# A two-layer graph-attention kernel: layer 2's softmax of large tiles in two halves, and the next tile's softmax six rows later

## The chip, the cores and the metric

The kernel runs on one core of one Trainium2 chip. The metric is the device time of one execution, in microseconds (us). Engines are named as the profile does: PE (matrix products), DVE (VectorE), ACT (ScalarE), POOL (GpSimd) and SP (the queue that issues plain transfers). PEld is PE's loading of weights.

## The reference

A graph with 10,000 nodes of 768 features and 170,000 directed edges (80,000 pairs in both directions and a loop on each node) goes through two attention layers. In each, a node's new row is a weighted sum of the rows of its neighbours:

```python
xl = (x @ W).reshape(n, heads, out_ch)
alpha_src = jnp.einsum('nhc,hc->nh', xl, a_src)
alpha_dst = jnp.einsum('nhc,hc->nh', xl, a_dst)
e = jax.nn.leaky_relu(alpha_src[src] + alpha_dst[dst], 0.2)
m = jax.ops.segment_max(e, dst, num_segments=n)
e = jnp.exp(e - m[dst])
s = jax.ops.segment_sum(e, dst, num_segments=n)
alpha = e / (s[dst] + 1e-16)
out = jax.ops.segment_sum(xl[src] * alpha[:, :, None], dst, num_segments=n)
```

Layer 1 has 4 heads of 256 features, layer 2 has one head of 768. After each layer comes a layer norm; layer 1 then has relu and adds `h0 @ Wr1 + br1`, layer 2 adds `h1 @ Wr2 + br2`. The input is added at the end, and a last layer norm follows. Everything is float32.

## The kernel before

The kernel first computes layer 1's table of rows and sorts the nodes by their number of incoming edges. The sorted nodes are cut into 79 tiles of 128 nodes; each node has one partition. A tile has as many *slots* as its busiest node has edges: 41, 27, 26, 25, 24, 24, 23 and so on down to 8. One slot is one row for each of the 128 nodes: a gather of 128 rows of 770 numbers (394 KB) from the table in HBM. The program keeps two paths; for this input the ordered one runs (`ordered_layer1`, then `ordered_layer2`).

`TURNS` sets the order in which tiles are worked: first every second tile from the smallest to the largest, then the others from large to small. I call the place in this order the *position*, t in the code of layer 2. Its slots go 8, 10, 11, 12, ... 22, 22, 23, 24 (position 37), 26 (38), 41 (39), 27 (40), 25 (41), 24, 23, 22, ... 9. In all there are 1377 slots.

The change is in layer 2 alone. There, a `Ring` in SBUF holds 41 rows (`RING2`). `ring.fetch(upto)` issues the gathers in order of slots: a tile's first row (the nodes' own rows) as a plain transfer on SP, all others as indirect transfers on POOL (L424). A slot of the ring can be filled again only when everything that reads its old row is done.

Position t of the loop does the following; the order of instructions on every engine is that of the Python text (`manual_schedule`), and each engine works its own list in order.

- `residual(t + 1)`: PE multiplies the next tile's `h1` by `Wr2` into a PSUM tile `rs[t + 1]` of two banks (L949, L952), and adds x by an identity product.
- `weights_of(t + 1)` is a generator that the loop starts in the middle of tile t. Its first part, `logits`, has DVE compute e for all slots of the tile (L477 reads the scores out of the ring's rows, then L188, L481, L484) and ACT its Exp (L485). Its second part has DVE normalise e (`normalised`, L496 to L499, after `doubled`, L502). Then for each row ACT makes a diagonal matrix of e (L937; 5 buffers of 4 diagonals), and PE multiplies it with columns 512 to 767 of the row (L938), summing in the free quarter of `rs[t + 1]`. A bias product (L933) goes before.
- Columns 0 to 511 are summed by DVE: one instruction for each row, `acc = row * e + acc` (L519, `weigh`), starting from the bias at the first row. After each, `ring.fetch` lets POOL issue one more gather.
- `norms(t - 1)`, the layer norms of the tile before, is stepped through at rows 0, 3, 6 and 9: statistics by DVE (L577, L579), `sd` by two ACT instructions (L581, L582), the scaling (L591, L593), the second norm, and the output row (L968), which POOL writes by an indirect transfer (L970).

The row at which the next tile's softmax starts is `turn`; its normalising stands three rows (`LEAD`) later:

```python
if t + 1 < NT and SLOTS[t + 1] + LEAD <= ring.size:
    ahead = weights_of(t + 1)
    turn = min(max(n // 3, n + SLOTS[t + 1] + 2 * LEAD - ring.size), n - LEAD)
```

The last gather of tile t + 1 is allowed by row `n + SLOTS[t + 1] - 41 - 1` of tile t, so the term in the middle puts the softmax six rows behind that. For the 41-row tile the condition fails: its weights are computed after the last row of the tile before.

Of the kernel before, what the change touches and what calls it, by code (L numbers as in the profile page):

```python
# [28 lines left out]
F32 = mybir.dt.float32  # L29
I32 = mybir.dt.int32  # L30
BF16 = mybir.dt.bfloat16
AF = mybir.ActivationFunctionType
OP = mybir.AluOpType
AX = mybir.AxisListType

P = 128
# [16 lines left out]
ON_PE1 = 4  # L53

# [25 lines left out]
def gnn_kernel(ctx, tc, x, x_cols, src, dst, src_col, dst_col, W1, a_src1, a_dst1, b1, g1, be1, Wr1, br1,  # L80
# [797 lines left out]
    def ordered_layer2():  # L878
        nonlocal ps_big
        with tc.tile_pool(name="b2", bufs=1) as pool, tc.tile_pool(name="small2", bufs=2) as small, \  # L880
# [39 lines left out]
            def whole(t):  # L920
                return SLOTS[t] <= ring.size

            def weights_of(t):


                n = SLOTS[t]
                ad = small.tile([P, H2], F32, name="ad")
                nc.vector.tensor_add(ad, ring.slot(FIRST[t])[:, C2:C2 + H2], lift)
                e, _ = logits(small, ring, FIRST[t], FIRST[t] + n, ad, H2, C2)
                yield e  # L930
                normalised(small, e, H2, t)
                to = rs[t][:, C2:2 * C2 - ON_PE2]
                nc.tensor.matmul(to, ones, b2_b[0:1, ON_PE2:], start=False, stop=False, skip_group_check=True)  # L933
                for k in range(n):
                    if k % G == 0:
                        diagonals = pool.tile([P, G, P], F32, name="diagonals", bufs=DIAGONALS)
                    nc.scalar.activation(diagonals[:, k % G, :], ident, AF.Copy, scale=e[:, k, :])  # L937
                    nc.tensor.matmul(to, diagonals[:, k % G, :], ring.slot(FIRST[t] + k)[:, ON_PE2:C2],  # L938
                                     start=False, stop=(k == n - 1), skip_group_check=True)
                yield  # L940

# [36 lines left out]
            ready = []  # L978
            assert all(whole(t) for t in range(NT))
            for t in range(NT):  # L980
# [4 lines left out]
                e = (ready or list(weights_of(t)))[0]  # L985
# [6 lines left out]
                if t + 1 < NT and SLOTS[t + 1] + LEAD <= ring.size:  # L992

                    ahead = weights_of(t + 1)
                    turn = min(max(n // 3, n + SLOTS[t + 1] + 2 * LEAD - ring.size), n - LEAD)
                for k in range(n):
                    if k in (turn, turn + LEAD):
                        ready += itertools.islice(ahead, 1)
                    if k in (LEAD, 2 * LEAD, 3 * LEAD):
                        next(last, None)  # L1000
                    weigh(acc, ring.slot(FIRST[t] + k), e[:, k], ON_PE2, None if k else b2_b)
# [3 lines left out]
                ready += ahead  # L1005
# [280 lines left out]
```

## Time and profile before

| | us |
|---|---|
| median of 3 runs | 5645.9 (5635.85 to 5646.04) |
| the profiled execution | 5629.25 |
| its span, first to last instruction | 5627.4 |
| busy in the span: PE, DVE, POOL, ACT | 4889.5, 4288.7, 3236.3, 2810.9 |
| L424, gathers of both layers, 2675 | 2655.8 (993 ns each) |
| L519, row times weight plus sum, 2530 | 1578.4 (624 ns each, two shapes) |
| L938, PE's part of the rows, 2754 passes | 742.1 (428 ns each) |

The profile is one execution's record. Its slices cut the span into 40 equal parts of 141 us; each digit is a share in tenths. Layer 2 fills the last fifteen and a half. A line of the timeline has the start, the length, the engine, the line of the kernel and the operation, then output<-inputs, the number of instructions merged into the line, and in brackets how long the engine had been idle and what ended that. A line of the waits has engine, its line, what it waited for, then the sum, the number of waits and the longest. PE's ends are modelled, so a wait "for PE" is read by the waiting engine's start, not by PE's record. "issue" and "remote" name idle time for which the record shows no instruction that ended it.

### The profile page before, as it was taken

The page shows a single profiled execution, that of the slowest core. Times are in us where ns is not written, and L with a number is a line of the kernel's source. Part 1 is how long each engine was busy: PE and PEld are TensorE (multiplying, and loading weights), DVE is VectorE, ACT ScalarE, POOL GpSimd, SP SyncE. Part 2 cuts the span into 40 slices and gives each one's busy share as a digit, 9 for nine tenths or more (in the row PEclk, how much of TensorE's full clock was granted, in tenths as well). Part 3 has the DMA queues.
Part 4 walks back from the last instruction along what each step waited for, and adds up shares of the span by engine and source line. Part 5 has one row for each costly group of instructions (what it writes and reads, how often), then busy time and mean ns, then how long its engine had stood idle before and what let it go on. Part 6 is the DMA issues. An engine that isn't in the chain of part 4 may idle for free. (4 is left out here: it accounts for less than half of the span.)

```text
span 5627.4 us, 59568 instructions
## 1 busy us (share of the span) xinstructions
PE 4889.5 (87%) x15191; PEld 2895.8 (51%) x15191; DVE 4288.7 (76%) x7729; ACT 2810.9 (50%) x8184; POOL 3236.3 (58%) x3159
## 2 busy tenths in 40 slices
PE   8999996999999875789999999998887747788898
PEld 3444443555555543455555555565555534555565
DVE  5783344999998887888999995887676656767787
ACT  3443343777788776778877763332222222222232
POOL 2447364556666555566665543666565656666663
PEclk9999998999999987899999999998888878889999
DMA  4333626999999987899999986998888878888885
GB/s 155 122 99 87 92 89 243 327 338 350 361 363 364 347 318 263 317 346 357 366 356 354 337 292 246 330 337 313 294 301 286 282 242 291 307 300 305 304 328 201
DMA packets 474306, 1591.37 MB, mean 283 GB/s; under 512 B 118327, under 2 KB 122487, under 8 KB 473958
## 3 DMA queue, kind: packets, MB, share of 16 engines
q0 software_dynamic: 322384, 1286.62, 64.5%
q1 hardware_dynamic: 149520, 297.43, 15.7%
q10 hardware_dynamic: 2054, 3.42, 0.2%
q8 instruction: 128, 2.10, 0.1%
q14 instruction: 220, 1.80, 0.1%
HBM read 1431.80 MB, written 177.29 MB: 286 GB/s over the span
## 5 line engine op out<-in xcount | busy, mean ns | idle before, releaser
L424 POOL DMA_INDIRECT ring<-table,slots x2675 | 2655.8, 993 | 1791.0 <-issue 518.8
L519 DVE SCALAR_TENSOR_TENSOR acc<-ring,e,acc 128x512 f32<-128x512 f32 (+1 forms) x2530 | 1578.4, 624 | 148.0 <-PE acc L733 48.6
L508 ACT ACTIVATE ring<-ring,e 128x256 f32<-128x256 f32 x3284 | 1338.6, 508 | 1.4 <-issue 1.4
L515 DVE TENSOR_TENSOR acc<-acc,ring 128x1024 f32<-128x1024 f32 x801 | 985.6, 1230 | 71.4 <-DVE acc L519 1.4
L952 PE MATMUL big<-wr,w 128*128 128x512 f32 (+1 forms) x2464 | 878.9, 502 | 139.8 <-issue 137.9
L938 PE MATMUL big<-ring,diagonals 128*128 128x256 f32 x2754 | 742.1, 428 | 206.0 <-issue 159.2
L171 PE MATMUL big<-w,xT 128*128 128x512 f32 x1896 | 825.9, 597 | 27.0 <-DMA w<-in_W_dram 10.4
L171 PE MATMUL big<-wr,xT 128*128 128x512 f32 x1896 | 833.5, 596 | 0.2 <-issue 0.2
L826 PE MATMUL half<-w,hT 128*128 128x512 f32 (+1 forms) x2528 | 830.4, 486 | 0.0
L938 PEld LDWEIGHTS big<-ring,diagonals 128*128 128x128 f32 x2754 | 586.4, 216 | 364.9 <-issue 232.7
L952 PEld LDWEIGHTS big<-wr,w 128*128 128x128 f32 x2464 | 482.3, 197 | 499.9 <-issue 468.9
L937 ACT ACTIVATE diagonals<-ident,e 128x128 f32<-128x128 f32 x1377 | 424.3, 388 | 617.2 <-remote 227.0
L826 PEld LDWEIGHTS half<-w,hT 128*128 128x128 f32 x2528 | 477.8, 189 | 372.3 <-issue 333.2
L733 PE MATMUL acc<-ring,diagonals 128*128 128x256 f32 x1912 | 481.8, 410 | 209.4 <-ACT diagonals L727 203.8
L171 PEld LDWEIGHTS big<-w,xT 128*128 128x128 f32 x1896 | 362.0, 192 | 486.6 <-issue 466.3
L171 PEld LDWEIGHTS big<-wr,xT 128*128 128x128 f32 x1896 | 356.7, 192 | 420.6 <-issue 420.5
L733 PEld LDWEIGHTS acc<-ring,diagonals 128*128 128x128 f32 x1912 | 388.8, 206 | 295.4 <-ACT diagonals L727 225.0
L581 ACT ACTIVATE sd<-mv,eps 128x1 f32<-128x1 f32 x237 | 69.4, 293 | 709.9 <-DVE mv L579 398.4
L727 ACT ACTIVATE diagonals<-ident,e 128x128 f32<-128x128 f32 x956 | 293.0, 387 | 204.2 <-DVE e L499 171.9
L665 DVE TENSOR_TENSOR scr<-big,ad_b 128x1024 f32<-128x1024 f32 x79 | 96.7, 1224 | 379.9 <-ACT row L662 348.1
L670 POOL TENSOR_TENSOR row<-row,none 128x1024 f32<-128x1024 f32 x79 | 187.1, 2368 | 266.6 <-ACT row L662 264.6
L485 ACT ACTIVATE e<-e 128x68 f32<-128x68 f32 (+29 forms) x160 | 38.2, 239 | 567.0 <-DVE e L484 302.0
(173 smaller groups left out, 3635.0 us busy)
## 6 DMA issues: line engine op xcount, KB each, us to landing
ring<-table,slots POOLq DMA_INDIRECT x2675
table<-row SPq DMA_DIRECT2D x79, 516.0 KB
h_d<-hT SPq DMA_DIRECT2D x79, 512.0 KB
w<-h_d SPq DMA_DIRECT2D x77, 512.0 KB
table<-row SPq DMA_DIRECT2D x79, 385.0 KB
ring<-table SPq DMA_DIRECT2D x79, 385.0 KB
xT<-in_x_cols_dram SPq DMA_DIRECT2D x79, 384.0 KB
x_d<-xt SPq DMA_DIRECT2D x79, 384.0 KB
```

Source lines behind the costliest of these rows:

```text
L171: nc.tensor.matmul(p[:, c:e], aT[:, j, :], w[:, j, c:e], start=(j == 0), stop=(j == k - 1))
L424: nc.gpsimd.indirect_dma_start(out=to, out_offset=None, in_=table, in_offset=bass.IndirectOffsetOnAxis(ap=index, axis=0), **more)
L508: nc.scalar.activation(row[:, s], row[:, s], AF.Copy, scale=e[:, h:h + 1])
L515: nc.vector.tensor_add(acc[:, :c], acc[:, :c], row[:, :c])
L519: nc.vector.scalar_tensor_tensor(acc[:, s], row[:, s], e[:, h:h + 1], (acc if first is None else first)[:, s], op0=OP.mult, op1=OP.add)
L670: nc.gpsimd.tensor_add(row[:, :C1], row[:, :C1], b1_b)
L727: nc.scalar.activation(diagonals[:, k * H1 + i, :], ident, AF.Copy, scale=e[:, k, i:i + 1])
L733: nc.tensor.matmul(acc[:, c:d], diagonals[:, k * H1 + i, :], ring.slot(q + k)[:, c:d], start=(k == 0 and c % BANK == 0), stop=(k == m - 1 ...
L826: nc.tensor.matmul(q, hT[:, j, :], w2[:, j, c:c + q.shape[1]], start=(j == 0), stop=(j == K1 - 1))
L937: nc.scalar.activation(diagonals[:, k % G, :], ident, AF.Copy, scale=e[:, k, :])
L938: nc.tensor.matmul(to, diagonals[:, k % G, :], ring.slot(FIRST[t] + k)[:, ON_PE2:C2], start=False, stop=(k == n - 1), skip_group_check=True)
L952: nc.tensor.matmul(r[:, c:d], hT[:, j, :], wr2[:, j, c:d], start=False, stop=(j == K1 - 1 and d < C2), skip_group_check=True)
```

## The change

Tiles of 26 and more rows (`PARTED2`: positions 38, 39 and 40 with 26, 41 and 27 rows) get their softmax in two halves with a running maximum. The first half's weights are exponentials under the first half's maximum, not normalised. Before row `cuts[1]` of the tile itself, `logits` of the second half takes the maximum of both; `fade` = exp(old maximum - new one) scales what was summed so far: DVE scales `acc` (and adds the bias there), ACT scales PE's quarter of `rs[t]` in place in PSUM. The second half's weights and the fade carry the whole sum's reciprocal. The second half's logits stand three rows before the cut, the normalising one row before.

For all tiles `turn` gets `4 * LEAD` in place of `2 * LEAD`, needs only the next tile's first half in the ring (`cuts_of(t + 1)[1]`), and stands behind the tile's own cut. The condition on the ring's size is gone, so the 41-row tile's first half is computed in the loop of the 26-row tile.

```diff
@@ -51,6 +51,7 @@
 ON_PE2 = 512
 SHARE = 4
 ON_PE1 = 4
+PARTED2 = 26
 
 
 def chunk_counts(n_edges):
@@ -917,27 +918,58 @@
             ones = pool.tile([1, P], F32, name="ones")
             nc.vector.memset(ones, 1.0)
 
-            def whole(t):
-                return SLOTS[t] <= ring.size
+            def cuts_of(t):
+
+                n = SLOTS[t]
+                return [0, n // 2, n] if n >= PARTED2 else [0, n]
 
             def weights_of(t):
 
 
-                n = SLOTS[t]
+                n, at, cuts = SLOTS[t], FIRST[t], cuts_of(t)
                 ad = small.tile([P, H2], F32, name="ad")
-                nc.vector.tensor_add(ad, ring.slot(FIRST[t])[:, C2:C2 + H2], lift)
-                e, _ = logits(small, ring, FIRST[t], FIRST[t] + n, ad, H2, C2)
-                yield e
-                normalised(small, e, H2, t)
+                nc.vector.tensor_add(ad, ring.slot(at)[:, C2:C2 + H2], lift)
                 to = rs[t][:, C2:2 * C2 - ON_PE2]
-                nc.tensor.matmul(to, ones, b2_b[0:1, ON_PE2:], start=False, stop=False, skip_group_check=True)
-                for k in range(n):
-                    if k % G == 0:
-                        diagonals = pool.tile([P, G, P], F32, name="diagonals", bufs=DIAGONALS)
-                    nc.scalar.activation(diagonals[:, k % G, :], ident, AF.Copy, scale=e[:, k, :])
-                    nc.tensor.matmul(to, diagonals[:, k % G, :], ring.slot(FIRST[t] + k)[:, ON_PE2:C2],
-                                     start=False, stop=(k == n - 1), skip_group_check=True)
+
+                def summed(e, lo, hi):
+                    for k in range(lo, hi):
+                        if (k - lo) % G == 0:
+                            diagonals = pool.tile([P, G, P], F32, name="diagonals", bufs=DIAGONALS)
+                        nc.scalar.activation(diagonals[:, (k - lo) % G, :], ident, AF.Copy, scale=e[:, k - lo, :])
+                        nc.tensor.matmul(to, diagonals[:, (k - lo) % G, :], ring.slot(at + k)[:, ON_PE2:C2],
+                                         start=False, stop=(k == n - 1), skip_group_check=True)
+
+                def add_b2():
+                    nc.tensor.matmul(to, ones, b2_b[0:1, ON_PE2:], start=False, stop=False, skip_group_check=True)
+
+                e, top = logits(small, ring, at, at + cuts[1], ad, H2, C2)
+                yield {0: (e, None)}
+                if len(cuts) == 2:
+                    normalised(small, e, H2, t)
+                    add_b2()
+                else:
+                    doubled(e, t)
+                    total = small.tile([P, H2], F32, name="total")
+                    nc.vector.reduce_sum(total, e.rearrange("p k h -> p h k"), axis=AX.X)
+                summed(e, 0, cuts[1])
                 yield
+                for lo, hi in zip(cuts[1:], cuts[2:]):
+                    e, new = logits(small, ring, at + lo, at + hi, ad, H2, C2, top)
+                    fade = small.tile([P, H2], F32, name="fade")
+                    nc.vector.tensor_sub(fade, top, new)
+                    nc.scalar.activation(fade, fade, AF.Exp)
+                    yield
+                    part = small.tile([P, H2], F32, name="part")
+                    nc.vector.reduce_sum(part, e.rearrange("p k h -> p h k"), axis=AX.X)
+                    nc.vector.scalar_tensor_tensor(total, total, fade, part, op0=OP.mult, op1=OP.add)
+                    nc.vector.tensor_scalar(total, total, 1e-16, None, op0=OP.add)
+                    nc.vector.reciprocal(total, total)
+                    nc.vector.tensor_mul(fade, fade, total)
+                    nc.vector.tensor_mul(e, e, total[:, None, :].to_broadcast([P, hi - lo, H2]))
+                    nc.scalar.activation(to, to, AF.Copy, scale=fade)
+                    add_b2()
+                    summed(e, lo, hi)
+                    yield lo, (e, fade)
 
             def residual(t):
 
@@ -975,34 +1007,51 @@
             q = product(brT, wr2, C2)
             rs = {0: residual(0)}
             last = iter(())
-            ready = []
-            assert all(whole(t) for t in range(NT))
+            ready, ahead = [], iter(())
+            assert max(SLOTS) <= ring.size
             for t in range(NT):
                 n = SLOTS[t]
                 if 0 < t < NT - 1:
                     rs[t + 1] = residual(t + 1)
                 h = parts[4 + t % 2][:, :C2]
-                e = (ready or list(weights_of(t)))[0]
+                if not ready:
+                    ahead = weights_of(t)
+                    ready += itertools.islice(ahead, 2)
+                es, later, cuts = dict(ready[0]), ahead, cuts_of(t)
                 acc = ps_acc.tile([P, BANK], F32, name="acc")
                 if not t:
                     rs[1] = residual(1)
                     ring.fetch(RING2)
                 next(last, None)
                 ready, ahead, turn = [], iter(()), n
-                if t + 1 < NT and SLOTS[t + 1] + LEAD <= ring.size:
+                if t + 1 < NT:
 
                     ahead = weights_of(t + 1)
-                    turn = min(max(n // 3, n + SLOTS[t + 1] + 2 * LEAD - ring.size), n - LEAD)
+                    turn = min(max(n // 3, cuts[-2] + 1, n + cuts_of(t + 1)[1] + 4 * LEAD - ring.size), n - LEAD)
                 for k in range(n):
+                    if k + LEAD in cuts[1:-1]:
+                        next(later)
+                    if k + 1 in cuts[1:-1]:
+                        lo, es_lo = next(later)
+                        es[lo] = es_lo
                     if k in (turn, turn + LEAD):
                         ready += itertools.islice(ahead, 1)
                     if k in (LEAD, 2 * LEAD, 3 * LEAD):
                         next(last, None)
-                    weigh(acc, ring.slot(FIRST[t] + k), e[:, k], ON_PE2, None if k else b2_b)
+                    lo = max(c for c in es if c <= k)
+                    weights, fade = es[lo]
+                    row = ring.slot(FIRST[t] + k)
+                    if k == 0 and len(cuts) > 2:
+                        nc.vector.tensor_scalar(acc[:, :ON_PE2], row[:, :ON_PE2], weights[:, 0], None, op0=OP.mult)
+                    else:
+                        if k == lo and fade is not None:
+                            nc.vector.scalar_tensor_tensor(acc[:, :ON_PE2], acc[:, :ON_PE2], fade, b2_b[:, :ON_PE2],
+                                                           op0=OP.mult, op1=OP.add)
+                        weigh(acc, row, weights[:, k - lo], ON_PE2, None if k else b2_b)
                     ring.fetch(FIRST[t] + k + 1 + ring.size)
                     if t + 2 < NT and k == n // 2:
                         ins[t + 2] = fetch_x(t + 2)
-                ready += ahead
+                ready += itertools.islice(ahead, 2 - len(ready))
                 for _ in last:
                     pass
                 if not t:
```

## The prediction

> **What bounds the kernel now.** I read the page's slices first: layer 2 fills the span from 3.45 ms on, and in its middle PE falls from 9 to 4 tenths. The change acts only there, so I then read the stretch tile by tile (edges: first row product L519 of positions 34 to 41). Columns: stretch, length; then busy us and count of PE, PEld, DVE, ACT, POOL; granted clock, DMA share, GB/s.
>
> ```profile
> 4316.20:4350.30 34.10, 26.97 (x87) 18.13 (x86) 23.52 (x47) 8.78 (x28) 21.90 (x23) 0.85 0.85 295
> 4350.30:4386.00 35.70, 27.96 (x97) 19.16 (x95) 23.37 (x46) 8.77 (x28) 23.61 (x25) 0.86 0.86 301
> 4386.00:4423.40 37.40, 26.80 (x78) 18.18 (x78) 24.24 (x47) 10.24 (x33) 22.07 (x24) 0.77 0.83 286
> 4423.40:4461.30 37.90, 20.76 (x62) 12.26 (x61) 25.16 (x48) 7.61 (x24) 26.43 (x28) 0.76 0.93 327
> 4461.30:4520.20 58.90, 43.87 (x135) 27.83 (x135) 26.91 (x51) 5.92 (x19) 26.24 (x28) 0.79 0.73 208
> 4520.20:4583.50 63.30, 25.06 (x97) 20.75 (x96) 37.75 (x64) 18.61 (x62) 35.75 (x38) 0.67 0.73 249
> 4583.50:4631.40 47.90, 31.40 (x98) 21.44 (x97) 27.32 (x52) 12.05 (x40) 24.96 (x27) 0.79 0.71 245
> 4631.40:4665.30 33.90, 24.59 (x74) 14.47 (x72) 25.66 (x49) 8.96 (x29) 23.09 (x24) 0.80 0.94 321
> ```
>
> The rows per tile are 22, 22, 23, 24, 26, 41, 27, 25. The three tiles of 26 and more rows (lines 5 to 7) move 208 to 249 GB/s where their neighbours move 286 to 327. Next the ordinary cycle, from the timeline of 4300 to 4345:
>
> ```profile
> 4307.17 5.95 ACT L937 ACTIVATE diagonals<-ident,e 128x128 f32<-128x128 f32 x20 [3.02 <-PE big L952]
> ...
> 4313.54 0.69 PE L933 MATMUL big<-b,ones 1*128 1x256 f32 x2
> ...
> 4327.68 0.69 ACT L937 ACTIVATE diagonals<-ident,e 128x128 f32<-128x128 f32 x2 [14.56 <-PE big L938]
> 4327.79 0.95 POOL L424 DMA_INDIRECT ring<-table,slots  x1 [3.74 <-PE big L938]
> ...
> 4328.82 1.02 DVE L593 SCALAR_TENSOR_TENSOR w<-w,sd,be 128x768 f32<-128x768 f32 x1 [9.32 <-ACT sd L582]
> ```
>
> ACT has 20 diagonal buffers; the last two of 22 diagonals wait for PE, and behind them stand the two sd instructions for which DVE waits 9.32 us. All three engines come free together at 4327, just after POOL's run of gathers stopped at 4324. So an ordinary tile is POOL issuing 1.25 us a row (0.95 busy and 0.30 between) and then a pause until PE's results arrive. DVE (23.5 busy of 34.1) and PE (27 of 34.1) have room. Seven ordinary tiles (positions 33 to 35 and 44 to 47: 151 rows, 234 us, counted the same way) give the pause: 234 - 151 x 1.25 = 45 us, 6.5 a tile. Then the waits from position 37 to 41, and DVE and PE around the 41-row tile:
>
> ```profile
> DVE e L477 <- DMA ring<-table,slots: 59.6, 6, 13.8
> POOL ring L424 <- DVE acc L519: 34.5, 17, 14.9
> POOL ring L424 <- PE big L938: 27.2, 7, 13.7
> DVE w L593 <- ACT sd L582: 26.5, 3, 10.1
> ```
> ```profile
> 4494.29 0.15 DVE L928 TENSOR_TENSOR ad<-ring,lift 128x1 f32<-128x1 f32 x1
> 4507.16 0.22 DVE L477 TENSOR_TENSOR e<-ring,ad 128x35 f32<-128x35 f32 x1 [12.72 <-DMA ring<-table,slots]
> 4516.77 0.17 DVE L477 TENSOR_TENSOR e<-ring,ad 128x6 f32<-128x6 f32 x1 [9.38 <-DMA ring<-table,slots]
> ```
> ```profile
> 4519.56 20.49 PE L938 MATMUL big<-ring,diagonals 128*128 128x256 f32 x82 [6.38 <-ACT diagonals L937]
> 4539.98 0.69 PE L933 MATMUL big<-b,ones 1*128 1x256 f32 x2
> 4578.91 9.90 PE L938 MATMUL big<-ring,diagonals 128*128 128x256 f32 x36 [38.24 <-issue]
> ```
>
> The 41-row tile fills the whole ring: its softmax can't start until the last row of the tile before it is used up, so DVE stands 22 us, POOL meanwhile has nothing to fetch (14.9 us), and then POOL waits 13.7 us more for PE. The 27-row tile's softmax comes after row 33 of 41, so PE idles 38 us.
>
> **The change, part by part.** All sums are against the profiled execution (5629.25 us, span 5627.4). It lies 16.7 us below the median of the runs shown (5645.9); I put the difference onto the median.
>
> *Two halves for 26, 41 and 27 rows.* The 41-row tile now needs 20 rows in the ring at row 17 of the 26-row tile, and 41 only at its own row 17, some 13 us (17 x 0.78) after the last slot came free. The 22 us of DVE and the 38 us of PE lose their cause. What is late next is POOL's own cadence. Positions 37 to 41 are 143 rows: 143 x 1.25 + 5 x 6.5 = 211 us, against 37.9 + 58.9 + 63.3 + 47.9 + 33.9 = 241.9 now. Gain 31 us. DMA allows it: 143 rows of 394 KB and five tiles of 1.29 MB in and out are 62.8 MB, in 211 us 298 GB/s, below the 327 of line 4.
>
> *What the halves add.* Per tile some 11 small DVE instructions (0.15 to 0.2 each, rows L477 to L499) and one 128x512 pass over acc (0.78): 3 us, hidden under POOL while DVE has 8 us of waiting in a tile; uncovered they would cost 9 us for three tiles. On ACT one more Exp of e, an Exp of fade and the scaling of PSUM: below 0.3, 0.3 and about 0.5 us (L508's 128x256 is 508 ns). The scaling is the dear one: it waits for PE's first half, and behind it on ACT stand the second half's diagonals and the next tile's Exp, for which DVE waits. PE's bias product waits for it too, and POOL then for PE's release of rows. No row shows this wait. From below it is 0: PE has a residual (10.7 us in the ordinary tile) between the halves. From above it is another pause, 6.5 a tile, 20 for three. As PE's results came only when POOL paused (14.56 us for ACT above), I take half: 10 us.
>
> *Next tile's softmax six rows later.* The term goes from 6 to 12 rows after the last fetch. With max(n // 3, ...) it moves 13 tiles by six rows (positions 31 to 36 and 40 to 46; 20 to 27 rows), some twenty others of 17 to 21 rows by one to five, and none of 16 or fewer; positions 37 and 39, whose next tile is parted, come 7 and 8 rows earlier, and 38 gets a place in the loop. POOL's and SP's instructions keep their order exactly; what moves past row products are DVE's logits and normalising, ACT's Exp and diagonals, PE's L933 and L938. Six rows are 6 x 0.78 = 4.7 us. It takes away DVE's waits at L477 in the ordinary tiles, but POOL runs through these, so they pay only where POOL stopped as well: positions 36, 42 and 43 lie 2.2, 0.6 and 1.4 us above 1.25 n + 6.5. Gain 4. Its price is PE's slack. Diagonals begin at 4307.17 and PE turns to them at 4313.54: 6.4 us of slack, 1.7 left after the move. Positions 36 and 44 had 2 to 3 us and come about 2 us late; PE makes that up in its wait. From below 0, from above 4.7 us x 13 = 61 if no slack holds; I take 2, by the row shown.
>
> A rule against this part: the Trainium skill, "DMA: Bandwidth & Descriptors", Anatomy of one DMA, fits a GpSimd-issued transfer at 2.0 us plus bytes over 436 GB/s. That would be 2.9 us for 394 KB (an estimate from that page), so six rows would be ample and the move worth nothing, the 4 us above being 0. The trace differs: the last gather before L477's 4516.77 was issued at 4506.56, 10.2 us earlier, behind a queue of others.
>
> Sum: -31 + 10 - 4 + 2 = **-23 us**: 5606 on the profiled execution, **5623 on the median**, 0.4%.
>
> **The rivals.**
> *A: the second pause is paid in full, and once more in the 41-row tile.* For: POOL ran 38 gathers in the 41-row tile while PE's work was long done; now rows 20 to 40 are released only after the scaling. Against: the residual between. Time: -31 + 20 + 6.5 - 4 + 2 = -6, 5640, no change to tell.
> *B: slower, by PE's slack.* One mechanism: the later diagonals reach PE after its residual, and L938, and the rows it releases to POOL, run late in each of the 13 tiles. It decides once diagonals come later than 6.4 us; from there each us costs 13. At the full 4.7 a tile: +61 - 23 = +38, 5684; at half, +8, 5654. For: positions 36 and 44 have only 2 to 3 us. Against: POOL's pause, not PE, ends those tiles, and PE's crawl before 4327 is waiting that can absorb it. The skill's "TensorE: Matmul & The Clock Gate", What's actually happening, would make it worse: an idle window of about 3.4 us halves the clock. The granted clock agrees (0.67 in the tile with 38 us of idle, 0.85 in the ordinary one).
> *C: the gain is larger.* If the waits at tile ends shrink too because PE's work is spread more evenly (clock 0.85 instead of 0.67 to 0.79), each of the ten tiles of 21 to 25 rows saves up to 2.5 us: -23 - 25 = -48, 5598.
> *D: the change doesn't act, since the first half waits as well.* At row 17 of 26 the last needed row was asked for 12 row products ago: 9.4 us against 10.2, so at most 1 us is left. Counted with A.
>
> **How the numbers follow.** About 0.2% (11 us) is what this kernel's measurement can tell from no change. Forecast 0.50, C 0.11, A with D 0.21, B 0.18. Faster: forecast and C, 0.61, plus a little of A, 0.62. Slower by more than 11 us is most of B and the worst of A: 0.17. Within: 0.21. The range runs from C with a few us of scatter (5594) to halfway into B (5666); about 0.1 lies above and 0.05 below. The forecast's own range is 5606 to 5635.
>
> **What would show it.** Right: DVE's wait for DMA at the logits line falls from 59.6 us at these positions to under 10; the 38 us gap of PE before the 27-row tile is gone; the 41-row tile keeps POOL above 0.85 of its cadence; positions 37 to 41 take 210 to 225 us. Wrong by A: ACT's scaling waits over 5 us for PE in each parted tile, and POOL waits for PE after some 20 gathers. Wrong by B: PE waits for ACT's diagonals after its residual in positions 31 to 46, and tiles of 20 to 25 rows, now 32 to 38 us, grow by 2 us or more.

## The result, and the profile after

| | kernel before | changed kernel |
|---|---|---|
| median, us | 5641.66 (5635.85 to 5646.04) | 5610.27 (5600.19 to 5623.55) |
| profiled execution, us | 5629.25 | 5608.18 |
| its span, us | 5627.4 | 5606.3 |

The ratio is 0.995, with a 95% interval of 0.9933 to 0.9968: the changed kernel is 31 us faster by the medians and 21 us by the two profiled executions. The forecast was 23 us less, 5623 us, with a range of 5594 to 5666.

Lines of the changed kernel stand one further down than before up to about L928 (gathers L425, logits L478, normalising L503, row product L520, scaling of the norm L594). In layer 2's loop, L938 is the diagonal matrices, L939 PE's rows, L943 the bias product, L969 ACT's scaling of PSUM at the cut, L981 and L984 the residual, L1048 DVE's scaling of `acc` at the cut.

These are the windows of the changed kernel, positions 34 to 41, each from its first row product to the next position's. Columns: stretch, length; then busy us and count of PE, PEld, DVE, ACT, POOL; granted clock, DMA share, GB/s.

```profile
4316.70:4350.90 34.20, 26.61 (x89) 17.86 (x88) 23.55 (x46) 8.80 (x29) 21.98 (x23) 0.85 0.86 298
4350.90:4384.30 33.40, 24.55 (x80) 16.55 (x79) 23.37 (x45) 7.98 (x26) 21.90 (x23) 0.85 0.85 295
4384.30:4419.40 35.10, 25.67 (x78) 16.98 (x77) 24.34 (x47) 8.27 (x28) 22.60 (x24) 0.83 0.85 295
4419.40:4453.70 34.30, 29.93 (x102) 21.40 (x102) 24.40 (x45) 10.62 (x35) 21.49 (x23) 0.88 0.84 285
4453.70:4492.90 39.20, 25.36 (x71) 15.56 (x71) 28.30 (x61) 11.73 (x38) 25.01 (x26) 0.74 0.85 304
4492.90:4549.00 56.10, 42.55 (x131) 27.75 (x130) 39.83 (x75) 14.42 (x48) 36.64 (x39) 0.80 0.95 304
4549.00:4596.40 47.40, 33.40 (x97) 21.35 (x96) 29.74 (x64) 12.58 (x41) 29.83 (x32) 0.73 0.85 286
4596.40:4636.50 40.10, 26.32 (x80) 17.13 (x79) 25.72 (x49) 7.23 (x24) 23.96 (x26) 0.82 0.78 272
```

The three tiles of 26, 41 and 27 rows (lines 5 to 7) now move 286 to 304 GB/s, as their neighbours do, in place of 208 to 249. The 26-row tile became 19.7 us shorter, the 41-row tile 7.2 us, the 27-row tile 0.5 us, and the 25-row tile behind them 6.2 us longer. Positions 37 to 41 together take 217.1 us in place of 241.9.

The waits of DVE and of POOL in those five positions (engine, its line, what it waited for, sum, times, longest):

```profile
DVE w L594 <- ACT sd L583: 20.1, 2, 11.2
DVE st L578 <- PE big L939: 14.4, 3, 7.2
DVE e L478 <- DMA ring<-table,slots: 8.4, 3, 3.5
...
POOL ring L425 <- PE big L939: 13.2, 15, 4.3
...
POOL ring L425 <- PE big L984: 9.1, 3, 7.3
POOL ring L425 <- DVE acc L520: 2.4, 8, 0.3
```

DVE's waits for gathers at the logits fell from 59.6 to 8.4 us. POOL's wait for DVE's row products fell from 34.5 us (longest 14.9) to 2.4. Its longest wait for PE's rows fell from 13.7 us to 4.3, but in total POOL waits for PE nearly as long as before: 25.9 us on three lines (L939, L984 and L981) in place of 29.8 on two. Waits that the record does not name rose from 2.5 to 10.5 us. So what the change took away is POOL's wait for DVE, not its wait for PE.

The logits of the 41-row tile in DVE's timeline of the changed kernel (start, length, engine, line, operation, output<-inputs; in brackets the idle time before and what ended it), its first half, and its second half in two instructions:

```profile
4476.72 0.19 DVE L478 TENSOR_TENSOR e<-ring,ad 128x20 f32<-128x20 f32 x1 [2.66 <-DMA ring<-table,slots]
4510.40 0.17 DVE L478 TENSOR_TENSOR e<-ring,ad 128x15 f32<-128x15 f32 x1
4515.26 0.17 DVE L478 TENSOR_TENSOR e<-ring,ad 128x6 f32<-128x6 f32 x1 [4.68 <-issue]
```

The two waits of 12.72 and 9.38 us have become 2.66 and 4.68. In PE's timeline the hole of 38.24 us ahead of the 27-row tile is gone, but PE crawls through the residual inside that tile:

```profile
4546.57 6.20 PE L939 MATMUL big<-ring,diagonals 128*128 128x256 f32 x18 [0.56 <-issue]
4552.61 1.02 PE L981 MATMUL big<-w,ident 128*128 128x512 f32 x2
...
4568.37 0.59 PE L984 MATMUL big<-wr,w 128*128 128x256 f32 x1 [1.53 <-issue]
4571.15 0.59 PE L984 MATMUL big<-wr,w 128*128 128x256 f32 x1 [2.20 <-issue]
4573.27 0.59 PE L984 MATMUL big<-wr,w 128*128 128x256 f32 x1 [1.53 <-issue]
```

From 4561 to 4578 PE does one pass every 2 to 3.5 us, and between them it waits for nothing that the record shows. ACT's three scalings at the cuts show what this holds up:

```profile
4469.38 0.45 ACT L969 ACTIVATE big<-big,fade 128x256 f32<-128x256 f32 x1 [2.25 <-remote]
4518.86 0.45 ACT L969 ACTIVATE big<-big,fade 128x256 f32<-128x256 f32 x1 [2.25 <-DVE e L968]
4580.34 0.45 ACT L969 ACTIVATE big<-big,fade 128x256 f32<-128x256 f32 x1 [17.90 <-remote]
```

2.25 us is ACT waiting for the few DVE instructions that make `fade`. Only the third scaling, in the 27-row tile, waited long. POOL issued 22 transfers without a pause from 4546.3 to 4573.6, one each 1.25 us; it next paused at 4575.3, and the scaling ran at 4580. But issuing alone is not enough to slow PE: for the first 14 us of that run PE kept its pace (18 passes from 4546.57 in 6.2 us, then 16 in 7.03).

Outside positions 37 to 41 one profile can't be read this finely. Positions 0 to 17, whose instructions the change leaves as they were, took 372.6 us before and 381.1 after.

### The profile page after: what moved, and what is told of

It is laid out like the page before. It is cut to its first block, busy times and chain, and to the rows that moved or that the text cites. A ratio compares the mean times of both kernels' runs of the same rounds, so it can differ in the third digit from the quotient of the medians.

```text
span 5606.3 us, 59619 instructions
## 1 busy us (share of the span) xinstructions
PE 4891.2 (87%) x15188; PEld 2894.9 (52%) x15191; DVE 4293.8 (77%) x7759; ACT 2814.9 (50%) x8193; POOL 3240.5 (58%) x3159
## 5 line engine op out<-in xcount | busy, mean ns | idle before, releaser
L425 POOL DMA_INDIRECT ring<-table,slots x2675 | 2659.3, 994 | 1767.9 <-issue 532.8
L520 DVE SCALAR_TENSOR_TENSOR acc<-ring,e,acc 128x512 f32<-128x512 f32 (+1 forms) x2530 | 1578.3, 624 | 148.6 <-PE acc L734 44.9
L984 PE MATMUL big<-wr,w 128*128 128x512 f32 (+1 forms) x2464 | 880.5, 503 | 142.4 <-issue 140.5
L939 PE MATMUL big<-ring,diagonals 128*128 128x256 f32 x2754 | 747.7, 430 | 172.5 <-issue 147.1
L939 PEld LDWEIGHTS big<-ring,diagonals 128*128 128x128 f32 x2754 | 590.0, 218 | 335.2 <-issue 215.2
L984 PEld LDWEIGHTS big<-wr,w 128*128 128x128 f32 x2464 | 482.3, 197 | 506.7 <-issue 475.4
L938 ACT ACTIVATE diagonals<-ident,e 128x128 f32<-128x128 f32 x1377 | 424.8, 388 | 603.3 <-remote 245.4
L669 ACT ACTIVATE scr<-scr 128x256 f32<-128x256 f32 x632 | 253.5, 402 | 120.3 <-DVE scr L666 120.3
```

The costliest lines, as they stand in the source:

```text
L425: nc.gpsimd.indirect_dma_start(out=to, out_offset=None, in_=table, in_offset=bass.IndirectOffsetOnAxis(ap=index, axis=0), **more)
L520: nc.vector.scalar_tensor_tensor(acc[:, s], row[:, s], e[:, h:h + 1], (acc if first is None else first)[:, s], op0=OP.mult, op1=OP.add)
L669: nc.scalar.activation(m[:, s], m[:, s], AF.Copy, accum_out=row[:, C1 + i * H1 + h:C1 + i * H1 + h + 1])
L938: nc.scalar.activation(diagonals[:, (k - lo) % G, :], ident, AF.Copy, scale=e[:, k - lo, :])
L939: nc.tensor.matmul(to, diagonals[:, (k - lo) % G, :], ring.slot(at + k)[:, ON_PE2:C2], start=False, stop=(k == n - 1), skip_group_check=True)
L984: nc.tensor.matmul(r[:, c:d], hT[:, j, :], wr2[:, j, c:d], start=False, stop=(j == K1 - 1 and d < C2), skip_group_check=True)
```

## The experiments

The theory: the gain is the ring's. The large tiles no longer stop POOL, so they run at POOL's cadence plus the ordinary pause. The rivals: the later softmax makes the gain; the scaling's wait takes a good part of it back; halves cost more than they bring in any tile that does not fill the ring. Each group of runs stands beside the kernel before on the same chip: the first four on one chip (before: 5636.55 us), the next three on a second (before: 5332.24 us), the last five on a third (before: 5634.01 and 5637.16 us). The chip of the first comparison is not on record. Ratios, not times, are compared between chips. All diffs are against the changed kernel, except where it says otherwise.

### The halves without the later softmax

```diff
-turn = min(max(n // 3, cuts[-2] + 1, n + cuts_of(t + 1)[1] + 4 * LEAD - ring.size), n - LEAD)
+turn = min(max(n // 3, cuts[-2] + 1, n + cuts_of(t + 1)[1] + 2 * LEAD - ring.size), n - LEAD)
```

> Halves as in the change, but the next tile's softmax stands six rows behind its last gather, as before the change. Theory (the gain comes from the parted tiles, POOL's cadence bounds the rest): 20 to 28 us below before, that is a ratio of 0.995 to 0.9965, and positions 37 to 41 take 215 to 228 us, although DVE waits for DMA again at the logits of the tiles of 22 to 25 rows, 3 to 8 us each. Rival (the later softmax brings the gain): less than 8 us below before, ratio above 0.9985.

5608.19 us, ratio 0.9953 (0.9937 to 0.9969): the whole gain of the change, as the theory had it. Positions 37 to 41 take 206.5 us, less than the 215 to 228 expected. Its three scalings waited 2.25 us each.

### The later softmax without the halves

Against the kernel before:

```diff
-turn = min(max(n // 3, n + SLOTS[t + 1] + 2 * LEAD - ring.size), n - LEAD)
+turn = min(max(n // 3, n + SLOTS[t + 1] + 4 * LEAD - ring.size), n - LEAD)
```

> The kernel before, with the next tile's softmax six rows later and no halves. Theory: within 8 us of before (ratio 0.9985 to 1.0015); DVE's waits for DMA at the logits are gone but for the 41-row and 27-row tiles, and the waits for sd at the end of the tiles grow by as much. Rival (the later softmax brings the gain): 15 us or more below before. Second rival (PE's slack is used up): 10 us or more above before, with PE waiting for ACT's diagonals after its residual.

5647.69 us, ratio 1.0019 (1.0007 to 1.0031): 11 us slower. So the theory (within 8 us) failed, and the size that the second rival named came true, but not by its mechanism: from 3500 to 5100 us PE's wait for the diagonals is 26.0 us before and 25.9 here. Positions 37 to 41 take 245.8 us, no less than before. The waits show what the move exchanges. Here are DVE's waits in layer 2 (3500 to 5100 us), first of the kernel before, then of this one:

```profile
DVE w L593 <- ACT sd L582: 108.4, 13, 10.1
...
DVE e L477 <- DMA ring<-table,slots: 84.5, 15, 13.8
...
DVE w L593 <- ACT diagonals L937: 7.7, 1, 7.7
```
```profile
DVE w L593 <- ACT sd L582: 144.0, 17, 14.4
...
DVE e L477 <- DMA ring<-table,slots: 40.6, 9, 12.9
DVE w L593 <- ACT sd L581: 31.4, 3, 11.9
```

The logits wait 44 us less, and the layer norm's scaling (L593) waits 59 us more: 175.4 in place of 116.1. The profiled execution, 5663.36 us, is the slowest of the eleven, so these waits are those of a long run. The reading is that the diagonals start later, so the last of them wait later for a free buffer, and the two sd instructions stand behind them on ACT.

Where this bites shows in positions 41 to 44 (25, 24, 23 and 22 rows). First the window of the halves alone, then that of the changed kernel, then DVE's longest wait in the latter:

```profile
4595.10:4733.60 138.50, 104.77 (x327) 66.25 (x327) 98.25 (x185) 36.40 (x116) 87.14 (x91) 0.85 0.86 296
```
```profile
4596.40:4742.80 146.40, 110.18 (x345) 74.60 (x344) 98.23 (x184) 35.98 (x116) 89.59 (x94) 0.84 0.81 286
```
```profile
DVE w L594 <- ACT sd L583: 41.0, 4, 11.4
```

The two kernels without the later softmax took 139.7 (before) and 138.5 us there (DVE's wait for sd: 14.8 plus 7.7, and 14.5). The five with it, with five buffers of diagonals and with no halves below 26 rows (this kernel, the change in two profiles, and the next two experiments), took 146.4 to 154.1 (the last in the slowest execution). Against that stand positions 35 and 36: 73.2 and 72.7 us without, 68.2 to 68.5 with the later softmax, some 4.5 us less.

### Halves for the 41-row tile alone

```diff
-PARTED2 = 26
+PARTED2 = 40
```

> As the changed kernel, but only the 41-row tile has two halves; the tiles of 26 and 27 rows have one softmax each. Theory: the 41-row tile's start is what mattered most (22 us of DVE and some 20 us of POOL), but the 27-row tile's softmax now has to wait until row 38 of 41, so PE idles again before it: 10 to 18 us below before, ratio 0.997 to 0.998, half of the change's gain. Rival (parting 26 and 27 rows only adds the scaling's wait): as fast as the changed kernel or faster, 30 us or more below before.

5623.41 us, ratio 0.998 (0.997 to 0.9991), 13 us against the 28 us of the halves for three tiles. Positions 37 to 41 take 221.2 us. Parting the one tile that fills the ring is worth about half, as the theory had it; parting the tiles of 26 and 27 rows beside it brings the rest. In positions 37 to 41 POOL still waits 26.3 us for DVE's row products, against 2.4 in the change, so the ring still runs out of free rows there.

### The scaling in PSUM left out

```diff
-                    nc.scalar.activation(to, to, AF.Copy, scale=fade)
```

> The changed kernel without ACT's scaling of PE's quarter of the sum in the three parted tiles (that part of the output is left unscaled between the halves). It prices the wait for PE that the scaling adds; in the changed kernel's profile it was 17.9 us once, in the 27-row tile, and 2.3 us in the two others. Theory (half of a pause each on average, 10 us): 5 to 12 us below the changed kernel, ratio to before 0.993 to 0.994, and the 27-row tile falls from 47.4 to about 41 us. Rival (the wait is hidden, the 47.4 us have another cause): within 4 us of the changed kernel.

5616.15 us, ratio 0.9963 (0.9948 to 0.9978). That is no faster than the change (0.995), so the theory of 5 to 12 us less failed. The long wait of position 40 went: 33.6 us there in place of 47.4. But position 39 took 66.4 in place of 56.1, and its end shows a pause of the same kind at another place, in the timelines of ACT and DVE of this kernel:

```profile
4551.85 0.40 ACT L938 ACTIVATE diagonals<-ident,e 128x128 f32<-128x128 f32 x1 [11.46 <-remote]
...
4556.08 0.43 DVE L578 BATCH_NORM_STATS2 st<-big 128x6 f32<-128x256 f32 x1 [12.34 <-remote]
```

The record does not name what ended these two waits; in the program the first needs a buffer that PE has read, the second a sum that PE has written. That the pause moved because the scaling is gone is not shown: in the second profile of the change, with the scaling, positions 39 and 40 took 61.6 and 37.4 us. Their sum hardly differs: 103.5 and 99.0 us in the two profiles of the change, 100.0 without the scaling. The pause comes in one place or another, whichever instruction meets it first.

### Seven buffers of diagonals with the halves alone

```diff
-DIAGONALS = 5
+DIAGONALS = 7
-turn = min(max(n // 3, cuts[-2] + 1, n + cuts_of(t + 1)[1] + 4 * LEAD - ring.size), n - LEAD)
+turn = min(max(n // 3, cuts[-2] + 1, n + cuts_of(t + 1)[1] + 2 * LEAD - ring.size), n - LEAD)
```

> As part_only (halves, softmax six rows behind the last gather), with seven buffers of four diagonals in place of five, so that ACT's last diagonals of tiles of 21 to 27 rows no longer wait for PE and DVE's 9 us wait for sd behind them can end early. Theory (a tile ends with POOL's pause, and DVE's wait lies under it): within 6 us of part_only, ratio to before 0.994 to 0.9965; DVE's time waiting at the sd line falls, and another wait of DVE or ACT for PE's results takes its place. Rival (DVE's wait for ACT is what sets the tile): 12 tiles lose up to 9 us each, 40 us or more below part_only.

5304.8 us, ratio 0.9946 (0.9932 to 0.9959) on the second chip. What it was to tell could not be seen there: on that chip DVE's statistics never wait for PE, and ACT's diagonals 2.2 us in 1500 (see the last section), so the buffers have nothing to relieve. The halves of the three large tiles alone were not run there with five buffers, so this ratio is not split between halves and buffers.

### Narrow rows in seven tiles

```diff
                 if q in self.own:
                     nc.sync.dma_start(self.slot(q), self.table[self.own[q] * P:(self.own[q] + 1) * P, :])
+                elif self.own and FIRST[42] <= q < FIRST[49]:
+                    gather(self.slot(q)[:, :77], self.table.rearrange("n (a b) -> (n a) b", b=77), slots[:, q:q + 1])
```

> The changed kernel, but the gathers of positions 42 to 48 bring 77 numbers a node in place of 770 (the rest of these rows is left as it was in the ring, so their output is not the reference's). POOL issues as many instructions as before. It asks what PE's crawl and late results hang on. If on POOL issuing without a pause: DVE's waits of about 9 us for sd stay, and positions 42 to 47 keep 33 to 38 us. If on the load of the DMA queues: PE runs without gaps, the waits for sd fall under 3 us, and a tile takes what DVE or POOL need, 27 to 30 us for 21 to 23 rows.

5265.89 us on the second chip (one time only, so without an interval), 66 us below the kernel before. The question was whether PE's late results come with POOL's issuing or with the traffic; they did not come late on this chip, so it stays open. The run shows another thing. From 4450 to 4600 us, all within the narrow tiles, this is the window of the kernel, and then DVE's only waits (this kernel's lines stand two further down than those of the change):

```profile
4450.00:4600.00 150.00, 138.66 (x516) 97.61 (x515) 141.51 (x269) 52.24 (x170) 114.03 (x119) 0.99 0.38 103
```
```profile
DVE w L596 <- ACT sd L585: 2.0, 2, 1.5
```

DVE is busy 141.5 of 150 us and never waits at the logits, and the DMA share is 0.38. With full rows in the same kernel (positions 33 to 36, 4148.6 to 4264.0) it is busy 93.8 of 115.4 us, and waits 16.7 us at the logits for gathers while the DMA share is 0.96. So on the second chip an ordinary tile ends with its gathers' transfers, and DVE is the next bound.

### Halves from 22 rows on, on two chips

```diff
-PARTED2 = 26
+PARTED2 = 22
```

> The changed kernel with halves for all tiles of 22 and more rows (12 tiles in place of 3). It prices the halves where there is no wait to take away. Theory (POOL's cadence bounds these tiles, a scaling that waits for PE now and then adds a pause): 0 to 20 us above the changed kernel, ratio to before 0.995 to 0.9985. Rival (halves help any large tile, since a softmax needs fewer rows in the ring): 10 us or more below the changed kernel.

5268.13 us, ratio 0.988 (0.9864 to 0.9895) on the second chip. The expected ratios fail, but they came from another chip, and the change itself was never run whole on this one. The kernel with narrow rows settles part of it: it is the change up to the start of position 40, before its narrow gathers begin. From layer 2's first row product to there, these are the windows of the halves of three tiles with seven buffers, of the change, and of halves from 22 rows on:

```profile
3458.60:4402.70 944.10, 848.48 (x2974) 577.90 (x2974) 804.01 (x1611) 300.70 (x957) 693.12 (x718) 0.95 0.97 358
```
```profile
3457.30:4376.00 918.70, 844.25 (x2963) 576.22 (x2964) 803.82 (x1611) 300.95 (x957) 692.11 (x715) 0.95 0.98 366
```
```profile
3460.70:4378.60 917.90, 843.82 (x2963) 575.27 (x2962) 810.02 (x1650) 304.02 (x969) 689.34 (x715) 0.95 0.98 367
```

So up to there the halves of the ordinary tiles gave nothing (0.8 us), against the rival, and the change is 25.4 us shorter than the halves alone (the two differ in the number of buffers as well, for which nothing waits there): DVE's waits for gathers at the logits are 80.7 us in the first, 60.5 and 54.6 in the others. On this chip it is the later softmax that gains, where on the first it lost 11 us. This is one profile of each kernel; positions 0 to 17, which are alike in all three, took 335.7, 335.9 and 336.2 us. What halves from 22 rows on bring behind position 40 there is not shown. The same kernel was run again on the third chip:

> The change with halves for tiles of 22 and more rows. Theory: on a chip where PE's results arrive at once, the halves free the ordinary tiles from the wait at the logits, so 5 to 30 us faster than the change itself in this group; on a chip where they come only in POOL's pauses, within 10 us of it, since POOL's cadence and the pause stay. Rival (a half costs its ten DVE instructions and a pause whatever the tile): 10 to 40 us slower than the change on either.

5609.78 us, ratio 0.9958 (0.9945 to 0.9971), and the change itself beside it:

> The change itself once more, beside the kernel before on the chip of this group. Theory now (two bounds): on a chip where PE's results reach ACT and POOL only when POOL's run of gathers pauses, an ordinary tile lasts 1.25 us a row and some 6.5 us, and the change gives a ratio of 0.995 as measured there. On a chip where they arrive at once, an ordinary tile ends with DVE's wait at the logits for the last gather; there the later softmax takes that wait away as well, in some 13 tiles of 4 to 7 us, so up to 50 us more than halves alone: a ratio of 0.985 to 0.990. Rival (only the three large tiles matter): 0.995 on either chip.

5617.74 us, ratio 0.9965 (0.9953 to 0.9977). So the change is worth 16 us on this chip and was worth 31 in the first comparison, with intervals that overlap; halves from 22 on are 8 us below it, within the 10 us expected for a chip of this kind, and the intervals overlap. The other half of the last expectation, that the later softmax gains where the results arrive at once, is borne out on the second chip as far as position 40; the ratio forecast for the whole change there was not measured.

### Halves from 18 rows on

```diff
-PARTED2 = 26
+PARTED2 = 18
```

> The change with halves for tiles of 18 and more rows, some twice as many tiles as at 22. Theory: where PE's results arrive at once, within 15 us of the halves from 22 on, since tiles of 18 to 21 rows leave the ring room enough already and no wait at the logits is there to be saved; where they come in POOL's pauses, 0 to 20 us slower than the change. Rival (halves help by shortening the path from the last gather to PE, whatever the size): as much again as from 26 to 22.

5601.43 us, ratio 0.9942 (0.9928 to 0.9957): 16 us below the change, where the theory had 0 to 20 us above it. The rival, that a half helps whatever the size, fits better: 8 us from 26 to 22, 8 more from 22 to 18. But the intervals of all three overlap, so neither step is shown by itself. DVE's extra instructions (4350.2 us busy in the span against 4293.8) cost nothing that can be seen.

### Seven buffers of diagonals with the whole change

```diff
-DIAGONALS = 5
+DIAGONALS = 7
```

> The change with 7 in place of 5 buffers of four diagonals, so that ACT can run 28 diagonals ahead of PE in place of 20, and the two sd instructions do not queue behind the last diagonals. Theory: where PE's results come in POOL's pauses, DVE's waits for sd (31.5 us in three waits at positions 37 to 40 of the change) go, but the tile still ends with POOL's pause, so within 10 us of the change; where they arrive at once, there are no such waits and it is within 6 us. Rival (the sd queue behind the diagonals is what ends the ordinary tile): some 30 tiles by 2 us or more, over 40 us faster.

5591.99 us, ratio 0.9924 (0.9911 to 0.9937): 26 us below the change, outside the theory's 10 and short of the rival's 40. Two things changed. Positions 41 to 44 take 139.0 us in place of 152.5, which is what the later softmax had cost there. But it is not shown that the queue behind the diagonals had been the whole cost. The diagonals hardly stop in these tiles any more (20 to 23 of them run through at once), and still DVE waits 33.2 us for sd there, against 47.5 in the change and 14.5 without the later softmax. What waits now is the second sd instruction, 3.99 to 8.20 us in each of the four tiles, as here in ACT's timeline:

```profile
4672.74 0.20 ACT L583 ACTIVATE sd<-sd 128x1 f32<-128x1 f32 x1 [7.47 <-remote]
```

In the program it needs nothing but the instruction before it, on the same engine. The last section comes back to it. And the pause no longer comes in every tile: here are the windows of positions 33 to 37 (21 to 24 rows) of this kernel.

```profile
4290.60:4315.10 24.50, 23.57 (x86) 16.48 (x85) 22.63 (x45) 6.53 (x21) 17.52 (x19) 0.96 0.92 327
4315.10:4353.70 38.60, 26.95 (x76) 17.03 (x76) 23.55 (x46) 11.10 (x36) 22.82 (x24) 0.78 0.81 286
4353.70:4381.50 27.80, 25.46 (x90) 17.83 (x89) 23.53 (x46) 7.82 (x26) 19.92 (x22) 0.93 0.91 330
4381.50:4421.60 40.10, 27.22 (x79) 17.23 (x79) 24.43 (x48) 9.58 (x32) 22.29 (x24) 0.76 0.80 283
4421.60:4447.10 25.50, 21.35 (x71) 14.97 (x70) 24.37 (x45) 7.20 (x23) 17.43 (x18) 0.86 0.84 276
```

The change takes 32.5 to 34.8 us for each of them, 169.9 in all. Here every second tile runs through in 24.5 to 27.8 us and the one after it pays; the sum is 156.5.

### Both: halves from 18 rows on and seven buffers

```diff
-DIAGONALS = 5
+DIAGONALS = 7
-PARTED2 = 26
+PARTED2 = 18
```

> The change with halves from 18 rows on and with 7 in place of 5 buffers of diagonals. Alone, on a chip where PE's results come in POOL's pauses, the one took 16 us off the change's median and the other 26. Theory (two causes: the halves free rows of the ring earlier, the buffers let ACT run further ahead of PE): they add to some 40 us, a ratio to the kernel before of 0.988 to 0.991 there. Rival (both are paid out of the same pause): no better than the buffers alone, 0.991 to 0.994. Where PE's results arrive at once, the buffers add nothing and the halves give what halves from 22 rows on gave, a ratio of about 0.988.

5588.51 us, ratio 0.9914 (0.99 to 0.9928), on the third chip too. That lies in the rival's range (0.991 to 0.994), but the interval reaches well into the theory's (0.988 to 0.991) and overlaps that of the buffers alone, so whether the gains add is not settled. It has the lowest median of the kernels run on that chip, 49 us below the kernel before.

## Why the prediction was right, and where its sum was not

**The halves.** Right, in mechanism and size. The forecast for positions 37 to 41 was 211 us by POOL's cadence and the pause, and 221 with the scaling; the trace has 217.1, and 206.5 without the later softmax. Tile by tile, 1.25 us a row plus 6.5 gives 36.5, 39.0, 57.8, 40.3 and 37.8; measured were 34.3, 39.2, 56.1, 47.4 and 40.1. The 27-row tile lies 7.1 us above, with its wait of 17.9 us in it, the 25-row tile 2.3, with DVE's wait for sd. How well the single tiles fit is luck: in the second profile of the change they took 34.8, 39.6, 61.6, 37.4 and 41.1 (214.5 in all), so the sum holds and the split does not. The sign that POOL would keep above 0.85 of its cadence in the 41-row tile held in both profiles (39 instructions in 56.1 us, 0.87; 44 in 61.6, 0.89). On the first chip the halves alone make the whole gain, and the later softmax alone makes none.

**What the halves add.** The 10 us for ACT's scaling were mis-sized, as half a pause in each of three tiles. Measured: eight of nine scalings (three executions) waited 2.25 to 3.19 us, mostly for DVE's `fade`, and one 17.9. So in three tiles the residual between the halves covers it as a rule, and leaving the scaling out gained nothing. A long wait there is no price in itself: with halves from 22 rows on, six of the twelve scalings on the third chip waited 6.3 to 15.3 us, and that kernel was not slower than the change; on the second chip, with the same kernel, none waited over 2.4. The DVE instructions were hidden, as forecast; even halves in every tile from 18 rows on were.

**The later softmax.** This step failed in its balance. The forecast was 4 us of gain at positions 36, 42 and 43 and 2 us of price, a net of -2; alone it measured +11. The gain came at 35 and 36 (4.5 us). The price came at positions 41 to 44: about 8 us in the change's first profile, 14 in its second. There the softmax comes late, and in the first profile the last diagonals of all four tiles wait 5.6 to 10.1 us with the sd instructions behind them. The prediction had read that queue in the ordinary cycle, but priced the move by PE's slack alone; it did not ask which wait a later run of diagonals makes longer. With seven buffers that price is gone (139.0 us), which supports the queue as its cause but does not show it: sd still came late there, for a reason that the record does not name. On the second chip, where ACT hardly waits for PE, the same move took 25 us off up to position 40; the prediction had read its bound from one chip. The Trainium skill, "DMA: Bandwidth & Descriptors", Anatomy of one DMA, would have made the move worth nothing, since six rows would be ample for a transfer of 2.9 us (an estimate from that page). The trace stands against it: twelve rows took 44 us of waiting from the logits, so six had not been ample. The move lost elsewhere.

**The rivals.** A, two full pauses: not borne out; three scalings with one long wait, and 217.1 us, not 234. B, slower by PE's slack: its sign holds for the later softmax alone, but not its mechanism; in positions 37 to 41 PE's wait for the diagonals fell from 19.5 us to nothing among its larger waits, and what grew was DVE's wait behind ACT. Of the tiles of 20 to 25 rows that it named, positions 33 to 36 and 42 to 46 did not grow by 2 us, and position 41 did, by 6. C, a larger gain, is not seen: positions 45 to 47 take 99.6 us before and 100.0 after.

**Between profile and median.** The forecast's -23 us lies between the -31 of the first comparison and the -16 of the third chip. Its sum came closer than its terms deserve, and in that there is luck: the halves with their scaling were put at -21 and alone gave -28, the later softmax at -2 and alone gave +11, so one error covers a part of the other.

## What to carry to other kernels

Where one tile fills a buffer to the last row, let its first step need only a part of it; what that is worth can be read beforehand as the tile's time above the cadence of its neighbours. Before moving a consumer later to spare it a wait, list what stands behind its work on every in-order queue, and price the longest wait that the move makes longer, here the sd instructions behind the last diagonals. Ask also which wait ends a tile on the machine at hand: the same move lost 11 us on one chip and took 25 us off the part of layer 2 that could be compared on another. A change of 0.5% is read from medians, beside the kernel before on the same chip: two executions of instructions that had not changed differed by 8 us in 18 tiles.

## What the runs showed of the hardware

The chips differ in what bounds this kernel. The kernel before took 5636.55 us on the first chip, 5634.01 on the third and 5332.24 on the second. The same kernel (halves from 22 rows on) shows the difference. Up to layer 2's first row product it took 3461 us on the second chip and 3467 on the third; nearly all of the 339 us between the two profiled executions lies in layer 2. First the second chip, then the third, each with the window from 4000 to 4500 us and then DVE's waits from 3600 to 5100, and for the third chip ACT's waits too.

```profile
4000.00:4500.00 500.00, 416.61 (x1431) 290.86 (x1430) 430.18 (x873) 159.84 (x519) 373.99 (x389) 0.90 0.97 352
```
```profile
DVE e L478 <- DMA ring<-table,slots: 85.6, 32, 10.2
```
```profile
4000.00:4500.00 500.00, 399.37 (x1268) 264.29 (x1269) 366.37 (x735) 136.68 (x434) 309.96 (x324) 0.86 0.87 296
```
```profile
DVE st L578 <- remote: 110.7, 15, 10.6
DVE st L578 <- PE big L984: 47.4, 6, 13.0
```
```profile
ACT diagonals L938 <- remote: 200.7, 31, 11.0
...
ACT diagonals L938 <- PE big L939: 100.2, 45, 13.7
```

On the second chip POOL ran 389 instructions in 500 us, one in 1.29 us, and DVE waited for little but gathers; neither DVE nor ACT had a wait for PE among the larger ones. On the third POOL ran 324, and ACT waited 100 us for PE before its diagonals and 201 us more at the same line for something that the record does not name. In the stops that I read in the timelines, POOL paused after runs of mostly 13 to 23 gathers, PE's results came through together, and ACT and DVE went on at the same moment, as in the cycle that the prediction shows.

Two things in the traces bear on why. The first: not only PE's results come late. In the seven-buffer kernel the second sd instruction, which by the trace waits for nothing but ACT's own counter of finished work (a semaphore), came 4.0 to 8.2 us late ten times in layer 2, as in the line shown above; on the second chip that never happened. The second: on the slow chips the record itself gets thin where POOL issues densely. On the second chip every instruction of PE, ACT and DVE that raises a counter has a record of it 0.02 us or less after its end. On the third, with the same kernel, 2% of them have none within 1 us where POOL had issued at most four transfers in the 10 us before, 23% where it had issued six and 69% where it had issued eight; the kernel before, in its first profile, has 1, 19 and 67%. Some of these records are lost and not late: 98 of the 158 second sd instructions there started without a record of the first. So it is not shown whether the counters are raised late, or whether the recording has part in the stops.

What the stops come from is open. Whether it is POOL's issuing, the traffic that goes with it, or PE's crawl for another reason, with POOL stopping for lack of free rows, was not told apart: the kernel meant for that, with the narrow rows, ran on the chip where none of this happened.
